# Copies of modulation vectors issued by ScalarE instead of SyncE in a fused Mamba and mixture-of-experts block

## The chip, the cores and the metric

The kernel runs on one core of a Trainium2 chip. A core has five engines that run their own instruction streams in order and wait for each other by semaphores: TensorE (PE, matrix products into PSUM), VectorE (DVE), ScalarE (ACT), GpSimd (POOL) and SyncE (SP, which here only issues DMAs). Sixteen DMA engines move the data that the streams ask for. The metric is the device time in microseconds, the median of several executions.

## The reference

The input x has 8 sequences of 512 tokens with 256 features. From a conditioning vector per sequence come six modulation vectors (shift, scale and gate for each of two halves of the block):

```python
mod = (_silu(L0_c) @ L0_wmod).reshape(L0_c.shape[0], 6, 1, -1)
sa, ca, ga, sb, cb, gb = (mod[:, i] for i in range(6))
ga, gb = (sign(g) * max(abs(g), 0.25) for g in (ga, gb))
h = _layernorm(x) * (1 + ca) + sa
x = x + ga * mamba(h)        # layer norm, projection, causal convolution, a 16-state scan, gate, projection
h = _layernorm(x) * (1 + cb) + sb
x = x + gb * experts(h)      # softmax router, top expert of 8, gelu MLP 256 -> 1024 -> 256, gate of the top two
```

The code above is cut and the Mamba and expert parts are only named. What matters here: `sb`, `cb` and `gb` are one row of 3 x 256 numbers for each sequence, and each token of the sequence needs that row in the second half.

## The kernel before, in words

The work has two phases, each with its own plan.

**First phase (stages of the Mamba half, lines 745 to 957).** A loop over the eight sequences b calls five stages. `stage_norm` loads the sequence (`xt`, by `load_x`, line 445, asked for two sequences ahead), normalizes it, modulates it with `bc` (the first three modulation vectors, line 751) and brings it to features by tokens (`xnT`). `stage_base` prepares the residual part. `stage_conv` projects four chunks of 128 features (`project`, line 736: two matmul groups into a PSUM tile `px`); ScalarE copies each `px` to `u` (line 827) and starts the convolution `sv` from it (line 828), VectorE adds three taps, and ScalarE applies Silu. Between them stands the scan: TensorE makes `pv` and three `pd`, and VectorE adds each to `v` (lines 800 and 818). `stage_out` projects four further chunks through the same `px` buffers, applies tanh (`tz`), multiplies `pc` from the states, and makes the output rows (`po`, `xr`) and the router's logits. The PSUM tag `px` has three buffers (`ps_x`, line 441); during the first sequence the products `pq`, from which `states` builds the matrix `cs` (line 623), use them too.

`stage_place` (line 914) writes the results of a sequence to a table in DRAM, `xp_d`, with one row of 1028 numbers for each token: 260 of its own (`OWN`: the new x, the statistics, the gate) and 768 of modulation (`OWN:ROW`). The first part is written from `xr` (line 924). For the second, line 928 has a DMA from DRAM to DRAM, which repeats the sequence's row of `modb_d` over 512 token rows: 1536 KB each, eight in all. Sequence 0's call asks for copies 0 and 1, and each later call b for copy b + 1. `modb_d` is written once, at line 520. All DMAs of this phase but the scatter of token numbers (`ids_d`, POOL) are issued by SyncE.

**Second phase (experts).** Token numbers sorted by expert are taken in slots of 256. POOL gathers the rows of `xp_d` for a slot (line 1074), SyncE loads the expert's weights, and two layers of matmuls follow.

**What sets the order.** `nc` is a `Plan` in both phases. A call such as `nc.scalar.activation` only records an operation, with the DRAM or tile regions that it touches. `Plan.order` (line 191) then places all operations: at each step it takes, over all engines, the operation that could start first, where the start is the latest of its inputs' ends and its engine's free time, and among equal starts the one with the nearest due time. A DMA costs its engine 0.4 in this arithmetic, whatever its size (line 110); its landing time is counted on one common wire (line 254), and those who need it follow 2.2 after that. Regions in DRAM are compared as flat ranges, so a copy n meets the xr write of the same sequence n, and no other. The due time of the copies is that of their stage, `(b + 3) * PERIOD` (line 1116). `emit` (line 280) issues the operations in the order of their planned starts, each on its own engine, and the engines keep that order.

Of the kernel before, what the change touches and what calls it, by code (L numbers as in the profile page):

```python
# [289 lines left out]
def adaln_mamba_moe_kernel(  # L290
# [15 lines left out]
    nc = tc.nc  # L306
# [30 lines left out]
    chip, nc = nc, plan  # L337
# [94 lines left out]
    with tc.tile_pool(name="wa", bufs=1) as wa, tc.tile_pool(  # L432
# [481 lines left out]
        def stage_place(t):  # L914

            b, xr, top, oh = (t[k] for k in ("b", "xr", "top", "oh"))
            gt = sm.tile([P, NT, 1], FP, name="gt")
            nc.vector.tensor_tensor(gt, top[:, :, 0:1], top[:, :, 1:2], ALU.subtract)
            nc.scalar.activation(gt, gt, AF.Tanh, scale=0.5)
            nc.vector.tensor_scalar(  # L920
                xr[:, :, D + 2], gt[:, :, 0], 0.5, 0.5, ALU.mult, ALU.add
            )
            nc.vector.memset(xr[:, :, D + 3 : OWN], 0.0)
            nc.sync.dma_start(
                out=xp_d[b * L : (b + 1) * L, 0:OWN].rearrange("(n p) c -> p n c", p=P), in_=xr
            )
            for n in range(b + 1 if b else 0, min(b + 2, B)):
                nc.sync.dma_start(
                    out=xp_d[n * L : (n + 1) * L, OWN:ROW], in_=modb_d[n].partition_broadcast(L)
                )  # L930


            sx = sm.tile([P, NT, E], FP, name="sx")
            nc.vector.tensor_copy(sx[:, 0, :], seen)
            for n in range(1, NT):
                nc.vector.tensor_tensor(sx[:, n, :], sx[:, n - 1, :], oh[:, n - 1, :], ALU.add)
            nc.vector.tensor_tensor(seen, sx[:, NT - 1, :], oh[:, NT - 1, :], ALU.add)
            pk = ps_t.tile([P, NT, E], FP, name="pk", tag="tp")
            for i, (m, r) in enumerate(((lower, oh), (ones, sx))):
                nc.tensor.matmul(  # L940
                    pk.rearrange("p n e -> p (n e)"), lhsT=m,
                    rhs=r.rearrange("p n e -> p (n e)"), start=(i == 0), stop=(i == 1),
                )
            at_ = sm.tile([P, NT, E], FP, name="at_")
            nc.vector.tensor_tensor(at_, pk, oh, ALU.mult)
            rowf = sm.tile([P, NT, 1], FP, name="rowf")
            nc.vector.tensor_reduce(rowf, at_, AX.X, ALU.add)
            row = sm.tile([P, NT], I32, name="row")
            nc.vector.tensor_copy(row, rowf[:, :, 0])
            for n in range(NT):  # L950
                with plan.wanting(done=[ids_d]):
                    nc.gpsimd.indirect_dma_start(
                        out=id_views[b * NT + n],
                        out_offset=bass.IndirectOffsetOnAxis(ap=row[:, n : n + 1], axis=0),
                        in_=tok[:, b * NT + n : b * NT + n + 1], in_offset=None,
                        bounds_check=E * TOK - 1, oob_is_err=False,
                    )
# [157 lines left out]
        for b in range(B):  # L1115
# [3 lines left out]
            stage_conv(t)  # L1119
            stage_out(t)  # L1120
            stage_place(t)
            if b == FEW - 1:
                nc.due = (B + 3) * PERIOD
# [30 lines left out]
    with tc.tile_pool(name="g", bufs=2) as gp, tc.tile_pool(  # L1154
# [186 lines left out]
        nc = chip  # L1341
# [62 lines left out]
```

## Time and profile before

| | us |
|---|---|
| median of 3 runs (590.71 to 592.6) | 592.2 |
| the profiled execution, its own time | 591.06 |
| its span, first to last instruction | 589.4 |
| first phase, about | 0 to 330 |

The mean granted TensorE clock of the profiled execution is 0.975. Here is how the answers of the profile that are used below are to be read. The page gives for each engine the busy time, its share of the span and the number of instructions. Its rows of forty digits show slices of 14.7 us each, where a digit is the busy share in tenths (for PEclk the granted share of TensorE's full clock, for DMA the mean busy share of the sixteen DMA engines). A timeline gives start, length, engine, source line, operation and "out<-in" by the program's names; a bracket at the end is the engine's idle time just before, and what ended it. Operations recorded through the plan all carry line 159 or 154, so they are told apart by their tiles. "SPq" is a DMA's issue by SyncE: its length is the time that the issuer was held, not the transfer's own time. The page's list of DMAs names these groups of the queue in question:

```profile
xp_d<-xr SPq DMA_DIRECT2D x8, 520.0 KB
xt<-in_x SPq DMA_DIRECT2D x8, 512.0 KB
bc<-mod_d SPq DMA_DIRECT2D x7, 384.0 KB
```

In the windows of the trace, TensorE is busy for 15.00 of the 15 us from 35 to 50, for 16.36 of the 17 us from 50 to 67, for 20.20 of the 23 us from 67 to 90 and for 36.47 of the 40 us from 90 to 130. VectorE is busy in these for 10.08, 15.97, 14.39 and 37.53 us, and ScalarE for 6.81, 8.99, 11.44 and 17.85 us.

### The profile page before, as it was taken

How to read it: one execution, taken by the hardware profiler on the slowest of the kernel's cores; microseconds unless marked ns; L12 is line 12 of the kernel's file. 1: busy time of each engine (PE TensorE's matmuls, PEld its weight loads, DVE VectorE, ACT ScalarE, POOL GpSimd, SP SyncE). 2: the span in 40 equal slices, each digit the busy share in tenths (PEclk: the TensorE clock that was granted, in tenths of full speed). 3: DMA queues.
4: the chain of work that ended last, by engine and by line, in shares of the span. 5: the costliest groups of instructions: out<-in, count | busy, mean ns of one | idle time of the engine just before them, and what ended most of it. 6: DMA issues, size and time to landing. Idle time of an engine off the chain costs nothing. (4 is left out here: it accounts for less than half of the span.)

```text
span 589.4 us, 8687 instructions
## 1 busy us (share of the span) xinstructions
PE 555.4 (94%) x2882; PEld 417.4 (71%) x2882; DVE 358.9 (61%) x1087; ACT 209.8 (36%) x404; POOL 207.9 (35%) x338
## 2 busy tenths in 40 slices
PE   5979997999999998999999898999999999999995
PEld 2544752756667573757658787888988988888895
DVE  5879958899796969688585923164243433522312
ACT  2318352635445553533341122213422222332140
POOL 1424270553636154453332420343242222322111
PEclk9869997999999998999999998999999999999999
DMA  7479985421210100001282979998887887786000
GB/s 271 145 189 248 269 243 120 65 64 36 61 41 0 38 1 22 16 0 38 62 271 58 250 176 397 392 407 281 280 272 268 277 254 246 270 289 195 15 18 21
DMA packets 58704, 96.73 MB, mean 164 GB/s; under 512 B 9852, under 2 KB 41854, under 8 KB 58656
## 3 DMA queue, kind: packets, MB, share of 16 engines
q1 hardware_dynamic: 50720, 72.98, 40.8%
q0 software_dynamic: 7936, 23.17, 11.3%
q8 instruction: 24, 0.39, 0.4%
q14 instruction: 24, 0.20, 0.1%
HBM read 86.42 MB, written 22.81 MB: 185 GB/s over the span
## 5 line engine op out<-in xcount | busy, mean ns | idle before, releaser
L159 ACT ACTIVATE gl<-ph,b1t 128x256 f32<-128x256 f32 (+1 forms) x152 | 68.4, 452 | 178.8 <-PE ph L154 144.9
L154 PE MATMUL py<-w2t,gl 128*128 128x256 f32 x476 | 109.1, 381 | 0.0
L154 PEld LDWEIGHTS py<-w2t,gl 128*128 128x128 f32 x476 | 91.2, 192 | 12.6
L159 PE MATMUL ph<-hT,w1t 128*128 128x256 f32 (+1 forms) x304 | 84.1, 358 | 3.2 <-ACT gl L159 1.6
L154 PE MATMUL ph<-hT,w1t 128*128 128x256 f32 (+1 forms) x304 | 84.2, 359 | 0.0
L159 DVE TENSOR_TENSOR ot<-py,b2t 128x256 f32<-128x256 f32 x34 | 14.4, 425 | 112.9 <-PE py L154 112.9
L159 DVE SCALAR_TENSOR_TENSOR sv<-u,pt,sv 128x512 f32<-128x512 f32 x96 | 76.3, 804 | 9.1 <-ACT sv L159 8.8
L159 POOL DMA_INDIRECT out<-ot,ids x36 | 36.2, 1006 | 129.3 <-DVE ot L159 119.7
L159 PE MATMUL px<-xnT,wi 128*128 128x512 f32 x128 | 72.4, 649 | 0.0
L154 PE MATMUL px<-xnT,wi 128*128 128x512 f32 x128 | 68.3, 616 | 0.0
L159 POOL DMA_INDIRECT xg<-xp_d,ids x36 | 39.5, 1097 | 73.1 <-DMA ids<-ids_d 27.4
L159 PEld LDWEIGHTS ph<-hT,w1t 128*128 128x128 f32 x304 | 54.7, 190 | 10.0 <-issue 2.2
L154 PEld LDWEIGHTS ph<-hT,w1t 128*128 128x128 f32 x304 | 55.5, 191 | 6.3
L154 PEld LDWEIGHTS px<-xnT,wi 128*128 128x128 f32 x128 | 25.5, 199 | 32.8 <-issue 32.8
L159 POOL DMA_INDIRECT ids_d<-tok,row x32 | 34.6, 1080 | 35.4 <-DVE row L159 26.3
L159 ACT COPY u<-px 128x512 f32<-128x512 f32 x32 | 18.7, 586 | 58.5 <-PE px L154 58.5
L159 PEld LDWEIGHTS px<-xnT,wi 128*128 128x128 f32 x128 | 22.0, 198 | 18.9 <-issue 16.6
L159 DVE COPY hT<-tp 128x512 f32<-128x512 f32 (+1 forms) x20 | 12.7, 635 | 36.9 <-PE tp L154 28.9
L159 ACT ACTIVATE tz<-px 128x512 f32<-128x512 f32 x32 | 19.1, 596 | 40.0 <-PE px L154 35.1
L159 POOL TENSOR_TENSOR rs<-ve,nhalf 128x4 f32<-128x4 f32 x16 | 19.2, 1203 | 34.8 <-DVE ve L159 33.7
L159 DVE TENSOR_TENSOR hg<-hg,xg 128x256 f32<-128x256 f32 x72 | 29.2, 424 | 1.1
L154 PE MATMUL pc<-v,cs 128*128 128x128 f32 x192 | 26.7, 275 | 0.0
(348 smaller groups left out, 924.6 us busy)
## 6 DMA issues: line engine op xcount, KB each, us to landing
w1t<-in_w SPq DMA_DIRECT2D x19, 1024.0 KB
w2t<-in_w SPq DMA_DIRECT2D x19, 1024.0 KB
xp_d<-modb_d SPq DMA_DIRECT2D x8, 1536.0 KB
xp_d<-xr SPq DMA_DIRECT2D x8, 520.0 KB
xt<-in_x SPq DMA_DIRECT2D x8, 512.0 KB
bc<-mod_d SPq DMA_DIRECT2D x7, 384.0 KB
b2t<-in_b SPq DMA_DIRECT2D x19, 128.0 KB
w<-in_w SPq DMA_DIRECT2D x2, 1024.0 KB
```

The lines of the kernel that those rows point to most:

```text
L154: me["calls"].append(lambda: getattr(getattr(self.nc, name), op)(*args, **kw))
L159: calls=[lambda: getattr(getattr(self.nc, name), op)(*args, **kw)],
```

## The change

The eight copies of line 928 are recorded on ScalarE instead of SyncE. Nothing else in the source differs: the sizes, the regions and the number of DMAs stay. The planner counts the 0.4 of each on ScalarE's time, and ScalarE's DMAs go into a queue of their own. Their place in ScalarE's order is found by the planner.

```diff
             for n in range(b + 1 if b else 0, min(b + 2, B)):
-                nc.sync.dma_start(
+                nc.scalar.dma_start(
                     out=xp_d[n * L : (n + 1) * L, OWN:ROW], in_=modb_d[n].partition_broadcast(L)
                 )
```

## The prediction

> **What bounds the kernel now.** I read the page first. TensorE is busy for 94% of the 589.4 us span; ScalarE, which gets the new work, for 36%.
>
> ```profile
> PE 555.4 (94%) x2882; PEld 417.4 (71%) x2882; DVE 358.9 (61%) x1087; ACT 209.8 (36%) x404; POOL 207.9 (35%) x338
> PE   5979997999999998999999898999999999999995
> PEclk9869997999999998999999998999999999999999
> DMA  7479985421210100001282979998887887786000
> ```
>
> TensorE (PE) is the bound almost everywhere, and the DMA engines are full only in slices 3 to 6 (29 to 88 us) and late. In the seventh slice (88 to 103 us) TensorE is busy for seven tenths only and its clock is at seven tenths. So a stall of TensorE anywhere before the end is added to the time, and one taken away is subtracted. Next the timeline of SyncE's queue (start, length, instructions; the seven copies between 35.34 and 66.62 asked one at a time):
>
> ```profile
> 33.19 0.29 SPq L159 DMA_DIRECT2D modb_d<-mod  x1
> 35.34 0.60 SPq L159 DMA_DIRECT2D xp_d<-modb_d  x1
> 35.98 0.61 SPq L159 DMA_DIRECT2D xp_d<-modb_d  x1
> 36.64 0.65 SPq L159 DMA_DIRECT2D xp_d<-modb_d  x1
> 37.33 5.19 SPq L159 DMA_DIRECT2D xp_d<-modb_d  x1
> 42.56 7.60 SPq L159 DMA_DIRECT2D xp_d<-modb_d  x1
> 50.21 8.28 SPq L159 DMA_DIRECT2D xp_d<-modb_d  x1
> 58.53 8.09 SPq L159 DMA_DIRECT2D xp_d<-modb_d  x1
> 77.46 0.40 SPq L159 DMA_DIRECT2D xt<-in_x  x1
> 96.11 0.51 SPq L159 DMA_DIRECT2D xp_d<-modb_d  x1
> ```
>
> The first three copies leave in about 0.6 us each, the fourth takes 5.19 us and the next three about 8 us each: the queue has taken in about 3.2 copies of 1.5 MB and then lets the issuer in only as fast as data drains. The eighth, with nothing in front of it, takes 0.51 us. SyncE can afford this; it computes nothing. Then what ScalarE does in those microseconds (timeline of ACT; the last bracket is idle time before, and what ended it):
>
> ```profile
> 40.53 0.59 ACT L159 COPY u<-px 128x512 f32<-128x512 f32 x1 [9.77 <-PE px L154]
> 41.02 0.78 ACT L159 ACTIVATE sv<-px,pt 128x512 f32<-128x512 f32 x1
> 44.42 0.59 ACT L159 COPY u<-px 128x512 f32<-128x512 f32 x1 [2.62 <-PE px L154]
> 44.91 0.79 ACT L159 ACTIVATE sv<-px,pt 128x512 f32<-128x512 f32 x1
> 45.71 1.28 ACT L159 ACT_TABLE_LOAD   x1
> 47.01 0.63 ACT L159 ACTIVATE sv<-sv 128x512 f32<-128x512 f32 x1
> 47.54 0.57 ACT L159 COPY u<-px 128x512 f32<-128x512 f32 x1
> ```
>
> These empty the three px buffers that TensorE's projections need. Last, what the copies do to others now (timelines of VectorE and of TensorE):
>
> ```profile
> 90.01 0.75 DVE L159 BATCH_NORM_STATS2 st<-xt 128x6 f32<-128x256 f32 x2 [7.96 <-DMA xt<-in_x]
> ...
> 91.74 0.35 PE L159 MATMUL pd<-v,wb 128*32 128x128 f32 x1 [2.57 <-DVE v L159]
> 92.75 2.07 PE L159 MATMUL px<-xnT,wi 128*128 128x512 f32 x2
> ```
>
> An xt issued at 77.46 lands at 90.0, behind copies in its own queue; VectorE stands 7.96 us, TensorE 2.57 us, and its next projection takes 2.07 us where the same pair takes 1.02 us warm (85.58 us).
>
> **Part 1: where the copies go on ScalarE.** The planner places an instruction at the earliest time that its inputs and engine allow, the nearer due time first at a tie. Copies 1 to 7 need only modb_d. In the plan of the kernel before (its own arithmetic, used for order alone) they are ready at 34.52. ScalarE's u and sv for the first projection run there from 33.80 to 35.36 and its second u starts at 37.64, a gap of 2.28. A copy is costed at 0.4, so six go into it (the sixth at 37.36), and the seventh into the next gap, after the second u, sv and first Silu and ahead of the third u. The order becomes u, sv, six copies, u, sv, Silu, one copy, u. Copy 0 waits for the first xr write and falls into an idle stretch (ScalarE stands 4.82 us before 102.36): nothing, and 2 us if the stretch is gone.
>
> **Part 2: what they cost there.** On SyncE each issue starts when the one before has been taken in; no row shows ScalarE issuing, and I take it that an activation behind a copy waits in the same way. One rule speaks against me: the Trainium skill, "DMA: Bandwidth & Descriptors", section "Issuing engines are not separate DMA queues", says that issuing from several engines saves only the issuer's time, usually small beside the transfer. Small would be the 0.51 us of copy 0: seven cost 3.6 us, nearly all in gaps. The rows above say 31.28 us for the same seven. I take the rows: same bytes, same shape, and the limit is what is still undrained. The two bounds of a copy are then 0.5 and 8.3 us.
>
> The six begin at 41.80, when the first sv ends. On an empty queue I give them the old spacing, 35.34 to 58.49 = 23.15 us, so they end at 64.95. The second u moves from 44.42 to 64.95: +20.5 us. Second u to Silu's end took 3.1 us, so copy 7 begins at 68.1; it can't be taken in before the drain allows, 8.13 us (58.49 to 66.62) after copy 6, at 73.1. The third u moves from 47.54 to 73.1: +25.6 us.
>
> Behind ScalarE: TensorE gets on until 50.35, where pq needs the buffer that the second sv frees (66.3), and its second pq that of the third sv (74.4). The next projection (53.04) waits for the fourth, at 76. VectorE's taps on the third u start at 74.4, after 48.82 before. It is dense from there to 55.2, where it makes the v that TensorE's pd of 55.54 reads, so that comes at 79.3 to 80.8. TensorE is late by 24 to 25.5 us. In 50 to 67 us TensorE is busy 16.36 of 17 us and VectorE 15.97, so nothing is caught up. Stalls of 16 and 7 us also leave the clock low (projections at 36.74 take 2.05 us), mostly hidden behind VectorE's lateness. I take +25.5 us.
>
> **Part 3: what SyncE's queue gives back.** SyncE loses eight issues. Its next DMA, bc at 73.17, waits for a buffer freed by work now later by the same 25 us, so the 6.5 us from 66.62 gain nothing by themselves. The xt load is what gains: issued at about 102, when the copies have drained (about 42.4 + 7 x 8.1 = 99), or sharing with the last. VectorE needs it at 82.06 + 25 = 107, and 0.5 MB in 4 to 5 us (an estimate from 195 to 250 GB/s and 2 us to land) arrives about then. So 7.96 us of VectorE's idle time go. For TensorE: the 2.57 us at 91.74, the slow px behind it (3.41 instead of 2.15 us: 1.2), waits of 1.26 and 0.53 us on VectorE at 97.37 and 98.31, and another slow pair at 98.66 (3.66 instead of 1.9: 1.7). At most 7.3 us, at least the 2.57. Next in line is TensorE itself, dense from 99 to 130. I take 6.5 us, because all these follow VectorE's lateness.
>
> Later xr writes need copy n landed in another queue; the second is issued at 133.37, long after 99: nothing (2 us of SyncE if that cover is gone, SyncE having 30 us waits there). POOL's gathers of xp_d begin at 289.1: nothing. Bytes and DMA time are unchanged. Small changes of the planner's order further on: 0, between -2 and +2 us.
>
> **Sum.** +25.5 - 6.5 = +19.0 us. The profiled execution's own time is 591.06 (span 589.4, 1.7 around it), so 610.1; it lies 1.1 below the median 592.2, and on the median the forecast is 611.2.
>
> **Rivals.**
> - *The queue does not hold ScalarE* (it takes all seven at 0.6 us, or the waiting happens outside the engine): then u comes 1.3 us later, hidden or not, and part 3 remains: -2.6 to -7.3, likeliest -5, about 587. This is the other side, and it turns on one number: how many copies ScalarE's queue takes in before it stands. At about five and a half the stall (25.6 us less 8.1 for each copy beyond 3.2) equals the gain; at seven it is gone. Against it is the 5.19, 7.60, 8.28, 8.09 series. For it: no row shows ScalarE issuing a DMA. Chance 0.07.
> - *Nothing comes back*: the xt still arrives late, since the copies run on to about 99 and later, or VectorE's idle time was not what held TensorE. +23 to +27, about 617. For it: the DMA engines are 87% busy from 67 to 90. Chance 0.17.
> - *ScalarE's queue is shallower*, so that a copy blocks from the second on: up to 2 x 8 us more, 620 to 628. Chance 0.06.
> - *The copies scatter* over later gaps, or the stall is half absorbed, as each pause lets the queue drain: +3 to +11, about 600. For it: the planner has gaps. Against it: ready copies are taken at the first. Chance 0.08. An exact balance, within 0.3%: 0.03.
> - *Forecast*: +12 to +23, 604 to 615. Chance 0.59.
>
> **Numbers.** The likeliest is 611. The range 600 to 621 takes in the forecast, nothing coming back and half of the scattered case. A measurement of this kernel can tell about 0.3% from no change: slower by more than that 0.90, within it 0.03, faster 0.07.
>
> **What would show it.** In the changed kernel: copies as ACT issues, four or five of 5 to 8 us; ScalarE without an activation from 42 to 65 us but for the first u and sv before it; TensorE idle some 20 us between 50 and 81 us, its releaser ACT or VectorE; the wait of VectorE on xt gone; px pairs after it at 1.02 us. Wrong, if the second u starts before 55 us, if the copies on ScalarE all last under 1 us, or if VectorE still waits over 4 us on an xt.

## The result and the profile after

| | before | after |
|---|---|---|
| median of 4 runs on the same chip, us | 591.46 | 608.37 (606.12 to 609.47) |
| the profiled execution, its own time, us | 591.06 | 608.26 |
| its span, us | 589.4 | 606.5 |
| mean granted TensorE clock | 0.975 | 0.964 |

The kernel became slower: ratio 1.0289, 95% interval 1.0261 to 1.0317. Forecast were +19.0 us, 611 (600 to 621) for the median and 610.1 for a profiled execution; measured are +16.9 between these medians and +17.2 between the two profiled executions. On TensorE, VectorE and GpSimd the instructions stand in the same order as before. ScalarE's order differs by the eight copies alone, SyncE's by their absence. So two instructions of the two traces can be paired one to one, and every shift below is the difference of two such start times.

First the page of after, cut; a slice is 15.2 us here, and the last line is the chain that ended last.

```profile
PE 555.8 (92%) x2882; PEld 415.9 (69%) x2882; DVE 361.1 (60%) x1087; ACT 209.9 (35%) x404; POOL 206.1 (34%) x338
...
PE   5983498899999999899999988999999999999996
...
PEclk9867599999999999999999999999999999999999
DMA  7449971531121010001064689999787887687000
...
PE 60%; DMA 17%; DVE 11%; ACTq 4%; issue 4%; POOL 2%; ACT 1%; SPq 1%; POOLq 0%
```

TensorE's busy time is the same to 0.4 us; the span is 17.1 us longer, so the time was lost standing. The row of PE shows where: slices 4 and 5 (45 to 76 us) read 3 and 4, where before they read 9. Slice 7, the hole of before, reads 8 instead of 7 (with later work in it). In the chain "ACTq", an issue by ScalarE, is now a step of its own, with 4% of the span, some 24 us.

The timeline of ScalarE in the kernel after, with its DMA issues (ACTq, each on a row of its own):

```profile
40.55 0.59 ACT L159 COPY u<-px 128x512 f32<-128x512 f32 x1 [9.04 <-PE px L154]
40.62 0.55 ACTq L159 DMA_DIRECT2D xp_d<-modb_d  x1
41.03 0.78 ACT L159 ACTIVATE sv<-px,pt 128x512 f32<-128x512 f32 x1
41.21 0.63 ACTq L159 DMA_DIRECT2D xp_d<-modb_d  x1
41.88 0.94 ACTq L159 DMA_DIRECT2D xp_d<-modb_d  x1
42.86 2.93 ACTq L159 DMA_DIRECT2D xp_d<-modb_d  x1
45.83 8.72 ACTq L159 DMA_DIRECT2D xp_d<-modb_d  x1
54.58 8.38 ACTq L159 DMA_DIRECT2D xp_d<-modb_d  x1
63.00 0.58 ACT L159 COPY u<-px 128x512 f32<-128x512 f32 x1 [21.19 <-DMA xp_d<-modb_d]
63.11 6.87 ACTq L159 DMA_DIRECT2D xp_d<-modb_d  x1
...
65.58 0.63 ACT L159 ACTIVATE sv<-sv 128x512 f32<-128x512 f32 x1
70.02 0.58 ACT L159 COPY u<-px 128x512 f32<-128x512 f32 x1 [3.81 <-issue]
```

Read the activations and the issues apart. The issues follow one another without a gap from 40.62 to 62.96: three of less than a microsecond, then 2.93, 8.72 and 8.38. The second u, which the program puts behind them, starts 0.04 us after the sixth ends; the third starts 0.04 us after the seventh ends (69.98). Before, these two u stood at 44.42 and 47.54, so they are late by 18.6 and 22.5 us.

What TensorE made of that (its timeline, then two windows: length, busy time and instructions of PE, PEld, DVE, ACT and POOL, then granted clock, DMA share, GB/s):

```profile
64.32 2.07 PE L159 MATMUL pq<-cmt,lt 16*128 16x512 f32 x2 [13.85 <-ACT sv L159]
71.34 2.07 PE L159 MATMUL pq<-cmt,lt 16*128 16x512 f32 x2 [4.95 <-ACT sv L159]
...
74.42 2.08 PE L159 MATMUL px<-xnT,wi 128*128 128x512 f32 x2
...
116.61 0.41 PE L154 MATMUL pk<-sx,ones 128*128 128x32 f32 x2 [1.27 <-DVE sx L159]
117.54 0.30 PE L159 MATMUL pd<-v,lm 128*32 128x128 f32 x1 [0.53 <-DVE v L159]
...
118.85 1.72 PE L154 MATMUL px<-xnT,wi 128*128 128x512 f32 x2
```

```profile
50.00:64.00 14.00, 0.47 (x5) 0.36 (x4) 0.00 (x0) 1.00 (x2) 0.00 (x0) 0.65 0.96 254
64.00:72.00 8.00, 2.73 (x3) 0.99 (x4) 3.67 (x9) 4.16 (x7) 3.36 (x3) 0.50 0.87 249
```

From 50 to 64 us hardly anything computes (PE 0.47 us, ScalarE 1.00) while the DMA engines are 96% busy: everything waits for a px buffer, hence for ScalarE, hence for the queue. TensorE stands 13.85 + 4.95 = 18.8 us, and the clock has fallen to half when it restarts (a px pair of 2.08 us, 1.13 before).

Last, VectorE at the place where it had stood 7.96 us for xt:

```profile
104.56 0.74 DVE L159 BATCH_NORM_STATS2 st<-xt 128x6 f32<-128x256 f32 x2
105.78 2.31 DVE L159 SCALAR_TENSOR_TENSOR xr<-mv,xr 128x4 f32<-128x4 f32 x1 [0.48 <-POOL xr L159]
...
108.35 2.09 DVE L159 TENSOR_TENSOR add<-xr,rsum 128x32 f32<-128x32 f32 x1
...
110.64 0.28 DVE L159 COPY v<-pv 128x128 f32<-128x128 f32 x1
```

The wait on xt is gone, but v, which TensorE's pd needs, comes 6.08 us after the st, where before it came 1.39 us after it (90.01 to 91.40). Two tiny operations take 2.31 and 2.09 us here. The same two in the kernel before, and then GpSimd in the kernel after:

```profile
90.68 0.15 DVE L159 SCALAR_TENSOR_TENSOR xr<-mv,xr 128x4 f32<-128x4 f32 x1
91.08 0.17 DVE L159 TENSOR_TENSOR add<-xr,rsum 128x32 f32<-128x32 f32 x1
```

```profile
105.72 2.35 POOL L159 TENSOR_TENSOR h<-h,xt 128x1024 f32<-128x1024 f32 x1
108.03 2.36 POOL L159 TENSOR_TENSOR wb__355<-wo,bc 128x1024 f32<-128x1024 f32 x1
```

The account of TensorE's shift, from paired starts:

| place (start before, after) | shift, us |
|---|---|
| second sequence's pv (80.93, 103.53) | +22.6 |
| its po, behind the gone xt wait (113.10, 132.28) | +19.2 |
| the fifth sequence's pk (236.90, 254.39) | +17.5 |
| the eighth sequence's pk, beside the first matmuls of the experts (325.63, 343.04) | +17.4 |
| end of the span | +17.1 |

### The profile page after: what moved, and what is told of

Read it like the earlier page. It is cut to its first block, busy times and chain, and to the rows that moved or that the text cites. A ratio compares the mean times of both kernels' runs of the same rounds, so it can differ in the third digit from the quotient of the medians.

```text
span 606.5 us, 8687 instructions
## 1 busy us (share of the span) xinstructions
PE 555.8 (92%) x2882; PEld 415.9 (69%) x2882; DVE 361.1 (60%) x1087; ACT 209.9 (35%) x404; POOL 206.1 (34%) x338
## 4 chain that ended last, share of the span: by engine, by line
PE 60%; DMA 17%; DVE 11%; ACTq 4%; issue 4%; POOL 2%; ACT 1%; SPq 1%; POOLq 0%
PE py L154 10%; DMA out<-ot,ids 8%; PE px L159 7%; PE po L154 7%; PE px L154 7%; PE ph L159 6%; PE ph L154 6%; DVE sv L159 4%; ACTq L159 4%; PE pc L154 4%; DMA ids<-ids_d 2%; PE po L159 2%; DMA ids_d<-tok,row 2%; DMA w1t<-in_w 2%; DMA xg<-xp_d,ids 2%
## 5 line engine op out<-in xcount | busy, mean ns | idle before, releaser
L159 DVE SCALAR_TENSOR_TENSOR sv<-u,pt,sv 128x512 f32<-128x512 f32 x96 | 74.7, 786 | 32.4 <-ACT sv L159 32.2
L159 PE MATMUL px<-xnT,wi 128*128 128x512 f32 x128 | 71.2, 639 | 0.0
L154 PE MATMUL px<-xnT,wi 128*128 128x512 f32 x128 | 67.8, 613 | 0.0
L159 PEld LDWEIGHTS px<-xnT,wi 128*128 128x128 f32 x128 | 21.7, 196 | 18.5 <-issue 17.4
L159 POOL TENSOR_TENSOR rs<-ve,nhalf 128x4 f32<-128x4 f32 x16 | 17.8, 1111 | 34.4 <-DVE ve L159 33.2
L159 POOL MEMSET u<- 128x3 f32 x32 | 2.9, 109 | 77.8 <-DVE sv L159 55.8
```

The source lines that it names most:

```text
L154: me["calls"].append(lambda: getattr(getattr(self.nc, name), op)(*args, **kw))
L159: calls=[lambda: getattr(getattr(self.nc, name), op)(*args, **kw)],
```

## The experiments

The theory: the copies cost what they hold. ScalarE may not start an activation behind an issue that the queue has not taken in, and the queue takes in only some three and a half copies at once. The gain, an earlier xt, is there as well, but smaller. Rivals: the engine or its queue is itself the harm (rather than the place in its order); each issue costs ScalarE something; the earlier xt gives nothing. All kernels keep the work and differ only in when the copies go out and on which engine; each ratio is against the kernel before on the same chip.

**No copy early, on either engine.** A condition makes each copy wait in the plan for the `xr` of its stage's sequence, so two go out with the first sequence and one with each later one, from 91 to 290 us. (The edits are shortened here; each replaces the `nc.sync.dma_start(` of before.)

```diff
+                with nc.wanting(done=[xr]):
                     nc.scalar.dma_start(   # e2: nc.sync
```

> All eight copies stay on ScalarE in its own queue, but each is recorded as needing its stage's xr, so the planner places one copy per sequence (two for the first) instead of six and one in a row. Nothing is left out. Theory (a full queue holds ScalarE): every copy is taken in within about 0.6 us, no hold, and the xt load no longer stands behind copies: 3 to 6 us below before, 586 to 588 us. Rival A (eight DMA issues on ScalarE, or a second queue beside SyncE's, cost by themselves): still 600 us or more. Rival B (what came back after the stall does not come from xt): no stall and no gain, 591 us.

> The same spreading with the copies on SyncE, as in the kernel before. Nothing is left out. Theory: the gain comes from not having seven copies ahead of the xt load, not from the queue, so about the same 586 to 589 us; up to 8 us of delay for an xt that meets one or two copies in the shared queue, probably hidden. Rival B: 591 us. Rival C (only a queue apart from SyncE's frees the xt): 591 us here and 587 with the copies on ScalarE.

**Some early.** Copies 1 to 5 (e3), or 1 to 3 (e4), as early as the plan likes; the others as in e1.

```diff
+                with nc.wanting(done=[] if 0 < n < 6 else [xr]):   # e4: n < 4
                     nc.scalar.dma_start(
```

> Copies 1 to 5 stay early on ScalarE between the first sv and the second u, copies 6, 7 and 0 come later, one per sequence. Nothing is left out. Theory: the hold ends when the fifth copy has been taken in, at about 54.6 us in the changed kernel's trace, so the second and third u are 10 us late, less the 5.5 us that came back: 595 to 597 us. Rival A (cost per early issue): five sevenths of 17 us, 603 to 604 us.

> Copies 1 to 3 early on ScalarE, the rest one per sequence. Nothing is left out. Theory: the queue takes in three without a hold (0.55 to 0.94 us each in the changed kernel), the second u is on time, and the gain on xt stays: 586 to 588 us. Rival A: three sevenths of 17 us, 598 to 599 us.

Measured: e1 599.16 (ratio 1.0103, 1.0032 to 1.0175), e2 600.79 (1.0140, 1.0077 to 1.0203), e3 606.66 (1.0239, 1.0154 to 1.0324), e4 598.9 (1.0102, 1.0079 to 1.0126). All four missed, three of them by over 10 us, and e4 landed where the rival of a cost per issue had put it (598 to 599). The shifts say that two things happened. At the pk of 297.93, near the end of the first phase, e1, e2 and e4 were ahead of the kernel before by 3.7, 4.0 and 4.0 us, about as expected, and e3 behind by 7.1. At the next pk, of 325.63, they stood at +3.4, +6.7, +7.6 and +17.3. Something between 298 and 326 us cost 7 to 12 us in each, also in e2, which issues nothing on ScalarE. In e2, SyncE's queue and VectorE there:

```profile
292.06 0.53 SPq L159 DMA_DIRECT2D xp_d<-modb_d  x1
294.21 0.40 SPq L1057 DMA_DIRECT2D w<-in_w  x1
```

```profile
315.11 0.41 DVE L159 TENSOR_SCALAR hg<-xg 128x256 f32<-128x256 f32 x1 [9.57 <-DMA xg<-xp_d,ids]
```

The last copy is issued 2 us ahead of the first expert weights and amid the first four gathers (xg, from 288.10). VectorE, working in order, stands 9.57 us for a gathered tile; before, it had no such wait there, and the same window has TensorE's po waiting 8.6 us for VectorE. My edit had moved the copies from one crowded place into another. That reading needed a test: the same early copies with the late ones elsewhere.

**Later copies moved ahead of the gathers.** The later copies wait for the `xr` of sequences 0, 1, 2 and 3, so all are out by about 200 us (in e7 of 0 to 2 and in e8 of 0 and 1, out by 166 and 142). Early are copies 1 to 3 on ScalarE (e5) and on SyncE (e6), 1 to 4 (e7) and 1 to 5 (e8) on ScalarE.

```diff
+            xrs[b] = xr
...
+                with nc.wanting(done=[] if 0 < n < 4 else [xrs[max(0, n - 4)]]):   # e7: 5, e8: 6
                     nc.scalar.dma_start(                                           # e6: nc.sync
```

> Copies on ScalarE: three early, then copies 0 and 4 with the first xr, 5, 6 and 7 with the second to fourth, so all are out before 210 us, far from the first gathers. Only the DMAs' places differ from the kernel before. In the first four runs every kernel without a hold was 3.7 to 4.1 us ahead of before until 298 us and lost 7 to 12 us between 298 and 326, when copy 7 went out at 290. Theory (front part: no hold, xt earlier; end part: late copies ahead of the first gathers): 587 to 588 us, 0.6 to 0.7% faster than before. Rival (the loss at 298 to 326 us comes with the earlier arrival, not with the late copies): 595 us or more again.

> The same places in time with all copies on SyncE's queue. Theory (the queue does not matter, only what stands in it and who issues): 587 to 589 us, within 1 us of the run with ScalarE. Rival (ScalarE's queue of its own is what frees xt): 591 to 592 us.

> As the first, with four copies early on ScalarE. Theory: the fourth is held 2.9 us, as in the changed kernel, the second u is late by 1.4 us: 588 to 590 us. Rival (a hold sets in with any fourth copy at the full pace of 8 us): 594 us or more.

> As the first, with five copies early on ScalarE and none late. Theory: the front part is that of the run before with five early, 7 us behind before at 298 us, and nothing is lost at 298 to 326: 598 to 599 us. With 608 for the changed kernel (six and one) and 588 for three, the time goes up by about 9 us for each copy beyond the fourth. Rival (loss grows with each issue on ScalarE): 591 to 595 us.

| kernel | median, us | ratio, 95% interval | start of second u | shift at pk 297.93 | at pk 325.63 |
|---|---|---|---|---|---|
| e5, three, ScalarE | 588.8 | 0.9956, 0.9936 to 0.9977 | 43.73 | -4.1 | -4.6 |
| e6, three, SyncE | 589.02 | 0.9954, 0.9933 to 0.9975 | | -4.1 | -4.6 |
| e7, four, ScalarE | 589.95 | 0.9971, 0.9954 to 0.9987 | 45.64 | -1.4 | -1.9 |
| e8, five, ScalarE | 597.92 | 1.0102, 1.0053 to 1.0150 | 53.97 | +6.5 | +6.0 |
| after, six and one | 608.37 | 1.0289, 1.0261 to 1.0317 | 63.00 | +18.0 | +17.4 |

The loss at 298 to 326 us is gone in all four, which confirms the reading of the first batch. What remains is a dose series: the number of early copies, on one engine, moves the second u and with it the time. The later copies also lie elsewhere in each, but at the pv of 80.93, ahead of all of them, the shifts are already -0.7 (e5), +2.0 (e7), +11.2 (e8) and +22.6 (after). ScalarE's timelines of e5 and of e8, the last early issue and the second u:

```profile
41.27 1.07 ACTq L159 DMA_DIRECT2D xp_d<-modb_d  x1
43.73 0.59 ACT L159 COPY u<-px 128x512 f32<-128x512 f32 x1 [2.53 <-PE px L154]
```

```profile
44.98 8.95 ACTq L159 DMA_DIRECT2D xp_d<-modb_d  x1
53.97 0.59 ACT L159 COPY u<-px 128x512 f32<-128x512 f32 x1 [13.00 <-issue]
```

With three, the last issue is over at 42.34 and u waits for TensorE, as before the change. With five, u starts 0.04 us after the fifth issue ends. That e5 carries all eight copies on ScalarE and e6 none, at the same time (588.8 and 589.02), refutes that the engine, its queue or the number of issues is the harm. And that both beat the kernel before shows that the xt gain is real and needs no change of engine. In e5, VectorE at the xt:

```profile
81.27 0.74 DVE L159 BATCH_NORM_STATS2 st<-xt 128x6 f32<-128x256 f32 x2
```

No wait precedes it, where before 7.96 us did. Of e5's 4.1 us, 0.7 are there by the pv of 80.93 (0.5 already at the px of 36.74, ahead of its first copy, so not by the copies) and 3.4 come at this place, the same 3.4 as in the kernel after (22.6 to 19.2). The medians of e5 and before differ by 3.3.

**What fills the queue.** The three early copies of e5 are each issued as two DMAs in one step of the plan, the bytes unchanged: by rows (256 rows of 768 numbers; e9), or by columns (512 rows of 384; e10).

```diff
+   for h in 0, 1:   # e9: rows h*256 to h*256+256, all 768 columns
+       chip.scalar.dma_start(...)   # e10: all 512 rows, columns h*384 to h*384+384
```

> As the run with three copies early on ScalarE, but each of the three is issued as two DMAs of 256 rows, so six DMAs with the same rows and bytes. It asks what the queue counts. If it counts rows or bytes: none is held (about 3 us for the six), the second u is on time at about 44 us, 588 to 589 us. If it counts DMAs (about four at a time): the fifth and sixth are held some 4 us each, second u at about 50 us, 594 us.

> As the run with three copies early on ScalarE, but each of the three is issued as two DMAs of 512 rows and half the columns, so six DMAs with twice the rows (3072) and the same bytes. If the queue counts bytes: no hold, second u at about 44 us, 588 to 589 us. If it counts rows (descriptors), it takes in some 1800 and then holds: the fourth to sixth DMA take 2 to 5 us each, together 8 to 12 us, second u at 50 to 54 us, 594 to 598 us.

Measured: e9 591.72 (1.0016, 0.9997 to 1.0035), e10 598.17 (1.0123, 1.0090 to 1.0157). ScalarE's timelines, the last of the six issues and the second u, of e9 and of e10:

```profile
45.47 2.01 ACTq L931 DMA_DIRECT2D xp_d<-modb_d  x1
47.52 0.59 ACT L159 COPY u<-px 128x512 f32<-128x512 f32 x1 [6.09 <-PE px L154]
```

```profile
49.43 5.59 ACTq L931 DMA_DIRECT2D xp_d<-modb_d  x1
55.06 0.59 ACT L159 COPY u<-px 128x512 f32<-128x512 f32 x1 [13.46 <-DMA xp_d<-modb_d]
```

From first issue to the end of the last, the same bytes hold ScalarE 2.3 us as three whole copies (40.00 to 42.34), 7.25 us as six halves by rows (40.23 to 47.48) and 14.6 us as six by columns (40.39 to 55.02). Bytes alone are refuted as the measure of capacity. Between e9 and e10 the bytes and the number of DMAs are the same, and the rows are twice as many and half as long: so the number of rows counts, or their length, which no run parts. Pieces by rows cost too, though rows and bytes are those of e5, so the number of DMAs counts somewhat, and the exact rule stays open. The times of these two tell less than the holds, because in both the profiled TensorE clock from 35 to 50 us was 0.53 and 0.54 (0.84 in e5): in e9 the second px pair itself took twice as long and ended at 47.36, so the hold to 47.48 cost the second u only some 0.1 us, and no pq waited for ScalarE. The clock rose at 49.17 and 48.81 there, and at 39.70 in e5; the last section comes back to that.

## Why the prediction was right, and where its terms were off

- **Order of the copies (part 1): right.** Six after the first sv, one after the first Silu, copy 0 between two tz, where ScalarE waits 3.83 us for TensorE; its issue ran ahead of the first of them (114.28, 0.48 us).
- **An activation behind a copy waits (the choice between 0.5 and 8.3 us a copy): right.** The steady issues are 8.72 and 8.38 us. The small price came true only for the first three. What the Trainium skill calls "usually small" ("DMA: Bandwidth & Descriptors", section "Issuing engines are not separate DMA queues") was small here while the queue had room: e5 shows that side (0.55 to 1.07 us), the kernel after the other.
- **Start and length of the hold: the term of +25.5 was too large.** The issues began at 40.62, not 41.80, because the issues did not wait for the activations ahead of them to end: the first runs beside the first u. The six took 22.34 us, not 23.15. Copy 7 began at 63.11, beside the second u, not at 68.1 behind the Silu, and ended 7.0 us after copy 6, not 8.13. These are 1.2 + 0.8 + 1.1 = 3.1 us, so the third u came at 70.02 instead of 73.1, and TensorE's lateness was 22.6.
- **What TensorE's lateness consists of.** The prediction hid the low clock behind VectorE. In fact 18.8 of the 22.6 us are standing; the remaining 3.8 fit the cold matmuls behind it: the two pq groups take 4.14 us against 1.96 for the four before, and the px of 74.42 and its partner 4.00 against 2.15, together 4.0 us more.
- **The next SyncE load moves with the rest: right.** bc was issued at 95.78, 22.6 us after 73.17; nothing was gained from SyncE's free time itself.
- **Recovery (part 3): 5.5 us in place of 6.5, by another sum.** At the xt wait 3.4 us came back, near the 2.57 and 1.2 that stood first in that sum. The waits of 1.26 and 0.53 us and the slow pair behind them, counted in as VectorE's lateness, stayed: 1.27, 0.53, and px pairs of 1.72 and 1.75. The step that failed is "all these follow VectorE's lateness". VectorE got 7.96 us back and lost 4.7 of them: without the wait, its small operations lie beside GpSimd's long ones. GpSimd's `h` runs from 105.72 to 108.07 and its `wb` from 108.03 to 110.39; VectorE's two operations end at 108.09 and 110.44, with them. Before, GpSimd had finished both by 87.79, while VectorE stood. The Trainium skill ("SBUF — State Buffer", section "Who interferes with whom") says that a VectorE operation with two SBUF inputs and a GpSimd operation that reads SBUF exclude each other for a whole instruction. The rows agree: the two take the time of the GpSimd operations (2.35 and 2.36 us) in the kernel after and in e5, and in the kernel before the same xr operation of the fifth sequence (227.32, beside an `h` of GpSimd from 227.25 to 229.60) takes 2.31 us. By the rows of before I had counted the two at 0.15 and 0.17. That the exclusion is the cause is argued from these rows, not tried alone.
- **The other 1.7 us, at 237, were luck; no term of the prediction has them.** Before, a pause was followed by slow px pairs, and in after an equal pause was not, because it lies otherwise to the steps of TensorE's clock (last section). e3, e8, e9 and e10 gain the same 1.7 us there; e5 does not (-4.1 on both sides). The last 0.4 us drift away later.
- **The sum.** 22.6 - 3.4 - 1.7 - 0.4 = 17.1 against 25.5 - 6.5 = 19.0. Both terms were too large, by 2.9 and, without the luck at 237, by 2.7. That these nearly cancel is luck too; the mechanism was right, the closeness of the number is better than its terms.
- **Rivals.** That the queue does not hold ScalarE fell on the rows above. Nothing coming back fell: the xt wait is gone here and in e5. A shallower queue fell: by estimate it takes some 3.65 copies (three, and the fourth at 2.93 of 8.4 us), more than the 3.2 read from SyncE. The copies didn't scatter. The other side existed where it was put: with fewer early copies the sign turns, between four (-1.4 us at the end of the first phase) and five (+6.5).

## What to carry to other kernels

Before a DMA is moved to an engine that computes, read how long its issue lasts where it is now, one by one: issues that last as long as the data take to drain, 8 us each here, show a full queue, and the new issuer stands for them with everything behind it. What was worth having here was fewer big copies at once, not another engine: three early and the rest spread over sequences 0 to 3 gave 588.8 us on ScalarE and 589.02 on SyncE, the first 0.44% below the kernel before (interval 0.23 to 0.64%) and the best version found. A copy that is put off has to land somewhere, and the first attempt put it beside the first gathers, where it cost 7 to 12 us.

## What the runs showed of the hardware that was not expected

- ScalarE's DMA issues and its activations overlap one way. An issue runs beside activations that stand ahead of it in the program (40.62 beside the u of 40.55; 63.11 beside u, sv, table load and Silu up to 66.2; copy 0 at 114.28, 1.9 us before the tz ahead of it started), but an activation behind an issue waits for its end (it starts 0.04 us after it: 63.00 and 70.02, and 53.97 in e8).
- The queue's room is not a number of bytes: 4.5 MB go in within 2.3 us as 1536 rows of 3 KB in three DMAs, and take 14.6 us as 3072 rows of 1.5 KB in six.
- An equal pause of TensorE may or may not lower its clock, by where it falls. Timeline of TensorE in the kernel before, then in after, at the same instructions:

```profile
230.88 0.30 PE L159 MATMUL pd<-v,lm 128*32 128x128 f32 x1 [1.87 <-DVE v L159]
...
232.57 1.92 PE L154 MATMUL px<-xnT,wi 128*128 128x512 f32 x2
```

```profile
250.06 0.30 PE L159 MATMUL pd<-v,lm 128*32 128x128 f32 x1 [1.89 <-DVE v L159]
...
251.38 1.02 PE L154 MATMUL px<-xnT,wi 128*128 128x512 f32 x2
```

  The pause is 1.87 us in one and 1.89 in the other; the pair behind it takes 1.92 us and 1.02 us. Two windows of before and one of after (granted clock third from the right):

```profile
228.38:231.79 3.41, 1.54 (x10) 0.48 (x9) 3.41 (x13) 0.60 (x1) 1.51 (x6) 1.00 0.00 0
231.79:235.20 3.41, 3.41 (x6) 1.35 (x5) 3.39 (x17) 0.80 (x2) 0.11 (x1) 0.50 0.10 37
```

```profile
248.74:252.15 3.41, 2.08 (x10) 1.02 (x11) 3.41 (x17) 0.28 (x2) 0.34 (x6) 1.00 0.00 0
```

  In all twelve traces of this case the granted clock changes in steps: each stretch at half clock lasts 3.41 us or a whole multiple of it, and the steps lie differently in each trace. Before, the pause (229.0 to 230.9) lies within one step, and the next step runs at half clock. In after, counted on in such steps from the last change at 122.46, one ends at 248.75, amid the pause (248.2 to 250.1), and the clock stays full. At this place all twelve agree: the pause of about 1.9 us lies within one step in seven (before, e1, e2, e4 to e7), with half clock behind it, and across two in five (after, e3, e8, e9, e10), without. At 36 to 40 us it fits as well: in ten traces the two px pairs fill a step, to 0.2 us, and the clock rises at its end; in e9 and e10 they lie across a boundary, and it rises later. That is read off these traces; no run moved a pause on purpose. A microsecond or two of a comparison between two traces can come from this alone.
